# Feed-forward weights turned by DMA transposes instead of TensorE, in a gated cross-attention block

## The chip, the cores and the metric

The kernel runs on one core of a Trainium2 chip. The time is device time in microseconds, as a median over repeated executions of the same program. Engines have short names: PE is TensorE (matmuls), DVE is VectorE, ACT is ScalarE, POOL is GpSimd, and SP is the engine that here only issues DMA transfers. A core also has 16 DMA engines.

## The reference

Sixteen batches of 224 tokens of width 512 attend to 750 context rows of width 384 with 8 heads, and then pass a feed-forward block whose activations and weights are quantised. Both parts are added to the input through a gate.

```python
x = x + tanh(g_xattn) * xattn(layernorm(x), ctx, mask, W_q, W_k, W_v, W_o, b_o)
x = x + tanh(g_ffn) * ffn(layernorm(x), w1, b1, w2, b2)

def weight_quant(w):            # w1 is 2048 x 512, w2 is 512 x 2048
    scale = 1.0 / clip(mean(abs(w)), 1e-5)
    return clip(round(w * scale), -1, 1) / scale

def bitlinear(x, w, b):         # act_quant: rows rounded to 8 bits
    return einsum('bsd,fd->bsf', act_quant(rmsnorm(x)), weight_quant(w)) + b

ffn = lambda x: bitlinear(gelu(bitlinear(x, w1, b1)), w2, b2)
```

The mean of the absolute weights is over the whole matrix, so all of a matrix has to be read before its first element can be rounded. The rounded weights are -1, 0 or 1.

## The kernel before, in words

The work goes batch by batch (the loop over `s` at L1505). For each batch the kept context rows are gathered and turned, keys, values and queries are computed, scores are taken in four units, and each unit passes through a chain of engines: PE computes the scores (L1047), DVE adds the mask and takes the maximum (L1061), ACT takes the exponential and its sum (L1071), DVE inverts the sum (L1080), POOL multiplies (L1081, the product `p`), PE turns the product (L1101 and L1108), and PE weighs the values with it (L1126, L1141). From batch 2 on the output projection (L1189), the first feed-forward matmul (L1259) and the second (L1304) of earlier token tiles are mixed in.

The feed-forward weights are prepared once, beside the first two batches. Each matrix is cut into eight chunks of 128x1024. `load_weights` brings a chunk in as f32 (512 KB; L1349 for w1, L1354 for w2), `sum_weights` adds up its absolute values, on DVE for even chunks and on ACT for odd ones (L1363, L1367), and `scale_weights` makes the scale when all eight are in. `round_weights` then rounds a chunk on DVE in three instructions, L1396 to L1398, the last two of which write a bf16 tile `w16`, taken from three buffers that carry the tag `xq`. `turn_weights` transposes it: eight transposes of 128x128 on PE (L1409 for w1, L1413 for w2) into one accumulator tile `wp`, and one eviction that casts it to fp8 into `w1T` or `w2T`. The accumulator tiles come from `gen`, four buffers that all other matmuls but the scores share.

`evict` (L757) puts each copy out of an accumulator on DVE or ACT, whichever has less planned work at that point; L763 is the copy on DVE, L766 that on ACT. In this program 15 of the 16 casts of turned weights fell to ACT.

`weight_pieces` makes a list of pieces with costs: in step c it rounds chunk c, and turns chunk c - 2. During batch 0 it works on w1, and each round is followed by the load of the same chunk of w2, into the buffer that the rounding has freed, and each turning by the sum over a chunk of w2. During batch 1 it works on w2. `merge` (L1434) mixes three lists, attention, the preparation of the next batch, and this one, so that each advances by the same share of its total cost.

This sets the order in which instructions are emitted. The order on an engine can differ from it, as the trace shows (L1519, emitted for batch 2, runs at 46.93 us, in batch 0): each engine has one queue, and an instruction that waits holds up all that is queued behind it.

The kernel already has transposing transfers on SP's queue: `normalise` turns the quantised activations with one (L1237, bf16, 128x1024, `xqT`), and `gelu` those of the hidden layer (L1288, 128x2048, `hqT`).

Of the kernel before, what the change touches and what calls it, by code (L numbers as in the profile page):

```python
# [9 lines left out]
BF16 = mybir.dt.bfloat16  # L10
# [715 lines left out]
def compact_path(ctx, tc, sh, x, context, out, late_loads):  # L726

    nc = tc.nc
    P = 128
    B, S, D = x.shape  # L730
    _, J, C = context.shape
# [5 lines left out]
    ND = D // P  # L737
# [8 lines left out]
    ident, ident16 = sh.ident, sh.ident16  # L746
    w1T, w2T = sh.w1T, sh.w2T
# [9 lines left out]
    def evict(dst, src, cols):  # L757

        kind = {"saturate": False} if dst.dtype == F8 else {}
        v, s = 80 + 1.2 * cols, 90 + 1.0 * cols  # L760
        if load["v"] + v <= load["s"] + s:
            load["v"] += v
            latest["v"] = nc.vector.tensor_copy(dst, src, **kind).ins  # L763
        else:
            load["s"] += s
            latest["s"] = nc.scalar.copy(dst, src, **kind).ins  # L766

    def gen(shape, dtype, name):
        return ps_gen.tile(shape, dtype, tag="gen", name=name)
# [403 lines left out]
    late = {}  # L1173
# [168 lines left out]
    def load_weights(wi, c):  # L1342

        raws[wi, c] = raw = late["raw"].tile([P, W], F32, tag="raw", name=f"raw_{wi}_{c}", bufs=NPC)
        if wi == 0 and c == 0:

            nc.scalar.copy(raw[0:1, 0:1], live[0]["ctx"][0:1, 0, 0:1])
        if wi == 0:
            return nc.sync.dma_start(  # L1349
                raw.rearrange("p (a d) -> p a d", d=D),  # L1350
                sh.w1_dram[c * 2 * P : (c + 1) * 2 * P, :].rearrange("(a p) d -> p a d", p=P),
            ).ins
        at = c % 2 * W
        return nc.sync.dma_start(raw, sh.w2_dram[c // 2 * P : (c // 2 + 1) * P, at : at + W]).ins  # L1354

    def sum_weights(wi, c):
        if c == 0:
            weight_sums.append(pa.tile([P, NPC], F32, name=f"wsums_{wi}"))
        if c == 1:
            late["junk"] = pa.tile([P, FF], F32, tag="h", name=f"junk_{wi}", bufs=2)  # L1360
        raw = raws[wi, c]
        if c % 2 == 0:
            nc.vector.tensor_reduce(  # L1363
                weight_sums[wi][:, c : c + 1], raw, AX.X, ALU.add, apply_absolute_value=True
            )
        else:
            nc.scalar.activation(late["junk"][:, :W], raw, AF.Abs, accum_out=weight_sums[wi][:, c : c + 1])  # L1367
# [3 lines left out]
    def scale_weights(wi):  # L1371
        tot = small(f"wtot_{wi}")
        nc.vector.tensor_reduce(tot[:, 0:1], weight_sums[wi], AX.X, ALU.add)
        pt = gen([P, 1], F32, f"wtotp_{wi}")
        nc.tensor.matmul(pt, lhsT=sh.ones, rhs=tot[:, 0:1], start=True, stop=True)
        mean = small(f"wmean_{wi}")
        nc.vector.tensor_scalar(mean[:, 0:1], pt, 1.0 / (FF * D), 1e-5, ALU.mult, ALU.max)
        sw = pa.tile([P, 1], F32, name=f"sw_{wi}")
        nc.vector.reciprocal(sw, mean[:, 0:1])
        isw = pa.tile([P, 1], F32, name=f"isw_{wi}")  # L1380
        nc.vector.reciprocal(isw, sw)
        if wi == 0:
            nc.vector.tensor_scalar(isw, isw, 1.0 / 127.0, None, ALU.mult)
        else:

            nc.vector.tensor_scalar(isw, isw, sh.tgates[:, 1:2], 1.0 / 127.0, ALU.mult, ALU.mult)
        weight_scale[wi] = sw
        sh.isw[wi] = isw
# [3 lines left out]
    def round_weights(wi, c):  # L1392

        raw = raws.pop((wi, c))
        quantised[wi, c] = w16 = pa.tile([P, W], BF16, tag="xq", name=f"w16_{wi}_{c}", bufs=3)
        nc.vector.tensor_scalar(raw, raw, weight_scale[wi], 1.0, ALU.mult, ALU.min)  # L1396
        nc.vector.tensor_scalar(w16.bitcast(I16), raw, -1.0, None, ALU.max)
        nc.vector.tensor_copy(w16, w16.bitcast(I16))  # L1398
        load["v"] += 1700

    def turn_weights(wi, c):
        w16 = quantised.pop((wi, c))
        pt = gen([P, 8, P], BF16, f"wp_{wi}_{c}")
        if wi == 0:

            for d in range(ND):
                for a in range(2):
                    at = a * D + d * P
                    nc.tensor.transpose(pt[:, 2 * d + a, :], w16[:, at : at + P], ident16)  # L1409
            evict(w1T[:, :, c * 2 * P : (c + 1) * 2 * P], pt.rearrange("p (d a) f -> p d (a f)", d=ND), 8 * P)  # L1410
        else:
            for f in range(8):
                nc.tensor.transpose(pt[:, f, :], w16[:, f * P : (f + 1) * P], ident16)  # L1413
            f = c % 2 * 8
            evict(w2T[:, f : f + 8, c // 2 * P : (c // 2 + 1) * P], pt, 8 * P)

    def weight_pieces(wi):

        p = []
        if wi == 1:  # L1420
            p += [(0.0, lambda: scale_weights(1))]
        for c in range(NPC + 2):
            if c < NPC:
                p += [(0.2, lambda c=c: round_weights(wi, c))]
                if wi == 0:
                    p += [(0.0, lambda c=c: load_weights(1, c))]
            if c > 1:
                p += [(0.6, lambda c=c: turn_weights(wi, c - 2))]
                if wi == 0:
                    p += [(0.0, lambda c=c: sum_weights(1, c - 2))]  # L1430
        return p
# [73 lines left out]
    for s in range(B):  # L1505
# [8 lines left out]
        if s < 2:  # L1514
            flow = weight_pieces(s)
        else:
            complete = 256 * (projected + 1) <= S * s
            if projected == 0:
                nc.gpsimd.tensor_scalar(sh.bo, sh.bo, sh.tgates[:, 0:1], None, ALU.mult)  # L1519
                nc.gpsimd.tensor_scalar(sh.b2, sh.b2, sh.tgates[:, 1:2], None, ALU.mult)  # L1520
            if complete:
                flow.append((0.0, lambda i=projected: residual(i)))
            if raised < projected:
                flow += up_pieces(raised)
                raised += 1
            if complete:
                flow += project_pieces(projected)
                projected += 1
                if lowered < raised:
                    flow += down_pieces(lowered)  # L1530
                    lowered += 1
# [53 lines left out]
```

## Time and profile before

| what | value |
|---|---|
| median of three runs | 757.25 us (756.26 to 759.62) |
| profiled execution | 755.32 us |
| its span | 753.5 us |
| mean granted PE clock in it | 0.976 |
| casts into w1T on ACT (L766) | 8, from 47.0 to 79.5 us, 1.02 us each |
| casts into w2T | 7 on ACT, 1.02 us each, and 1 on DVE, 1.22 us, from 90.3 to 114.1 us |
| transposes on PE | 64 (L1409) from 46.3 to 78.4 us, 64 (L1413) from 89.2 to 113.7 us, 219 ns each from start to end |

A transpose of 219 ns overlaps the next one, so that eight in a row occupy PE for 0.61 us. In the views of the trace an arrow `out<-in` names the tile written and the tiles read. A wait is named by the waiting instruction and the one that released it. PEld is the load of the stationary operand, which overlaps PE; SPq, POOLq and the like are the queues that issue. The chain is the sequence of work that ended last, followed back from the end of the program.

### The profile page before, as it was taken

The numbers are of one execution on the slowest core, as the hardware profiler recorded it, in microseconds if no ns is written. First come the engines' busy times: TensorE is split into PE (matmuls) and PEld (weight loads), VectorE is DVE, ScalarE is ACT, GpSimd is POOL, SyncE is SP. The second block draws the span as 40 slices with busy tenths as digits, with TensorE's granted clock in tenths as the row PEclk, the third lists the DMA queues.
The fourth block names the chain that finished last, engine by engine and source line by source line (L and its number), as shares of the span: only waits on it lengthen the run. The fifth ranks groups of instructions, "written<-read, shape, count | busy, mean of one in ns | idle before, by whom it ended". The sixth has DMA issues, their size and how long they took to land.

```text
span 753.5 us, 11378 instructions
## 1 busy us (share of the span) xinstructions
PE 680.1 (90%) x3902; PEld 432.9 (57%) x3902; DVE 505.9 (67%) x1300; ACT 407.6 (54%) x960; POOL 397.0 (53%) x543
## 2 busy tenths in 40 slices
PE   4997799999999999997999999999999999988652
PEld 3875587666566566555655575666666666443221
DVE  5598765877484784665768676588594939586860
ACT  1556564384663855736657369266565656460530
POOL 6583567464564644647266564565654453536141
PEclk9998999999999999999999999999999999999887
DMA  6874031132223322222142323123122222213150
GB/s 193 314 267 156 11 90 45 15 73 56 69 47 70 82 56 57 67 57 81 28 99 67 71 67 68 32 77 80 58 57 70 56 70 57 71 28 77 35 113 31
DMA packets 87218, 58.77 MB, mean 78 GB/s; under 512 B 75488, under 2 KB 75632, under 8 KB 87024
## 3 DMA queue, kind: packets, MB, share of 16 engines
q1 hardware_dynamic: 79024, 32.00, 18.8%
q0 software_dynamic: 8128, 25.96, 11.1%
q8 instruction: 33, 0.54, 0.3%
q14 instruction: 33, 0.27, 0.1%
HBM read 32.26 MB, written 7.34 MB: 53 GB/s over the span
## 4 chain that ended last, share of the span: by engine, by line
PE 57%; DVE 12%; issue 10%; POOL 9%; DMA 5%; ACT 2%; POOLq 0%; ACTq 0%; DVEq 0%; SPq 0%
PE qp L1008 9%; PE op L1189 9%; PE fp L1304 8%; PE hp L1259 6%; PE kp L892 5%; PE sim L1047 4%; PE vp L907 4%; PE ptp L1101 3%; PE av L1126 3%; DVE a L1282 2%; POOL p L1081 2%; DVE h L1267 2%; DMA raw<-in_L_ffn_w_dram 2%; DMA hqT<-hq 2%; DVE hq L1285 1%
## 5 line engine op out<-in xcount | busy, mean ns | idle before, releaser
L1081 POOL TENSOR_TENSOR p<-p,rec 112x768 f32<-112x768 f32 (+1 forms) x64 | 84.2, 1318 | 74.8 <-DVE rec L1080 29.6
L1304 PE MATMUL fp<-w2T,hqT 128*128 128x512 fp8e4 x448 | 104.2, 387 | 13.8 <-DMA hqT<-hq 13.7
L1259 PE MATMUL hp<-w1T,xqT 128*128 128x512 fp8e4 x448 | 107.0, 383 | 8.8 <-DVE h L1267 6.2
L1071 ACT ACTIVATE p<-p,nm 112x192 f32<-112x192 f32 (+1 forms) x256 | 106.4, 419 | 11.5 <-DVE nm L1061 11.3
L1008 PE MATMUL qp<-xnT,wq_sb 128*128 128x224 f32 x512 | 104.9, 358 | 0.6 <-ACT xnT L766 0.6
L1189 PE MATMUL op<-wo_sb,xoT 128*128 128x512 f32 x224 | 103.7, 599 | 0.0
L1008 PEld LDWEIGHTS qp<-xnT,wq_sb 128*128 128x128 f32 x512 | 96.8, 193 | 6.4 <-issue 3.3
L1267 DVE SCALAR_TENSOR_TENSOR h<-hp,c,b_bc 128x1024 f32<-128x1024 f32 x56 | 71.6, 1280 | 39.9 <-PE hp L1259 37.4
L1061 DVE CUSTOM_DVE_ANT_0 p<-sim,mask 112x192 f32<-112x192 f32 (+1 forms) x256 | 67.7, 319 | 33.9 <-PE sim L1047 33.4
L1304 PEld LDWEIGHTS <-hqT 128*128 128x128 bf16 x448 | 43.3, 99 | 71.0 <-DMA hqT<-hq 16.9
L1282 DVE TENSOR_REDUCE a<-h 128x1 f32<-128x2048 f32 x28 | 63.9, 2282 | 22.4 <-ACT h L1279 22.3
L1259 PEld LDWEIGHTS <-xqT 128*128 128x128 bf16 x448 | 43.2, 98 | 57.7 <-issue 15.4
L1308 DVE SCALAR_TENSOR_TENSOR y<-fp,c,y 128x512 f32<-128x512 f32 x28 | 20.9, 746 | 76.3 <-PE fp L1304 73.0
L1310 POOL DMA_INDIRECT out_dram<-y,token x28 | 30.9, 1104 | 75.6 <-DVE y L1308 70.6
L1290 ACT ACTIVATE h<-h 128x2048 f32<-128x2048 f32 x28 | 53.4, 1907 | 22.1 <-DVE hq L1285 14.7
L1279 ACT ACTIVATE h<-h 128x2048 f32<-128x2048 f32 x28 | 53.5, 1909 | 19.6 <-DVE k L1200 10.6
L1189 PEld LDWEIGHTS op<-wo_sb,xoT 128*128 128x128 f32 x224 | 40.6, 190 | 38.9 <-issue 36.4
L892 PE MATMUL kp<-ctxT,wk_sb 128*128 128x192 f32 (+1 forms) x384 | 60.9, 306 | 0.0
L892 PEld LDWEIGHTS kp<-ctxT,wk_sb 128*128 128x128 f32 x384 | 55.2, 192 | 6.2 <-issue 4.3
L1247 POOL TENSOR_TENSOR y<-y,b_bc 128x512 f32<-128x512 f32 x28 | 36.6, 1311 | 37.9 <-DVE fx L1228 37.6
L766 ACT COPY pT<-ptp 128x448 f32<-128x448 f32 x63 | 32.7, 536 | 42.6 <-PE ptp L1101 41.3
L1101 PE MATMUL ptp<-ident,p 112*128 112x112 f32 x256 | 36.1, 268 | 17.6 <-POOL p L1081 17.5
(165 smaller groups left out, 1191.4 us busy)
## 6 DMA issues: line engine op xcount, KB each, us to landing
raw<-in_L_ffn_w_dram SPq DMA_DIRECT2D x16, 512.0 KB, 5.6
wq_sb<-in_L_xattn_W_q_dram SPq DMA_DIRECT2D x1, 1024.0 KB, 5.8
b_bc<-in_L_ffn_b_dram SPq DMA_DIRECT2D x1, 1024.0 KB, 7.8
wk_sb<-in_L_xattn_W_k_dram SPq DMA_DIRECT2D x1, 768.0 KB, 7.4
wv_sb<-in_L_xattn_W_v_dram SPq DMA_DIRECT2D x1, 768.0 KB, 8.8
wo_sb<-in_L_xattn_W_o_dram SPq DMA_DIRECT2D x1, 512.0 KB, 3.8
wo_sb<-in_L_xattn_W_o_dram SPq DMA_DIRECT2D x2, 256.0 KB, 5.6
x<-in_x_dram,token POOLq DMA_INDIRECT x28, 3.6
```

The costliest lines, as they stand in the source:

```text
L892: nc.tensor.matmul(pk[:, p - p0, :], lhsT=sh.wk[:, c, p * P : (p + 1) * P], rhs=st["ctxT"][:, c, :cap], start=(c == 0), stop=(c == NC - 1),)
L1008: nc.tensor.matmul(pq[:, i, :], lhsT=sh.wq[:, d, (p + i) * P : (p + i + 1) * P], rhs=st["xnT"][:, d, :], start=(d == 0), stop=(d == ND - 1),)
L1061: nc.vector.tensor_tensor_reduce(out=probs[:, h, :cap], in0=sim[:, j, i, :cap], in1=st["mask"][:, j * begin : j * begin + cap], scale=-(DH ...
L1071: nc.scalar.activation(probs[:, h, :cap], probs[:, h, :cap], AF.Exp, bias=nmax, scale=-1.0, accum_out=total[:TQ, h : h + 1],)
L1081: nc.gpsimd.tensor_tensor(probs[:, :, :cap], probs[:, :, :cap], rec[:TQ].unsqueeze(2).to_broadcast([TQ, 4, cap]), ALU.mult,)
L1101: nc.tensor.transpose(pt[:, h, :], probs[:, h, c : c + P], ident[:TQ, :TQ])
L1189: nc.tensor.matmul(po, lhsT=xoT[:, d, at : at + P], rhs=sh.wo[:, d, :], start=(d == 0), stop=(d == ND - 1))
L1259: nc.tensor.matmul(ph[:, n, :], lhsT=f["xqT"][:, k * ND + d, :], rhs=w1T[:, d, at : at + NB], start=(d == 0), stop=(d == ND - 1),)
L1267: nc.vector.scalar_tensor_tensor(h[:, cols], ph.rearrange("t i n -> t (i n)"), f["c1", k], sh.b1[:, cols], ALU.mult, ALU.add)
L1279: nc.scalar.activation(f["h", k], f["h", k], AF.Gelu)
L1282: nc.vector.tensor_reduce(amax[:, k : k + 1], h, AX.X, ALU.max, apply_absolute_value=True)
L1304: nc.tensor.matmul(po, lhsT=f["hqT", k][:, n, :], rhs=w2T[:, n, :], start=(n == 0), stop=(n == NF - 1))
```

## The change

In `turn_weights` the eight transposes on PE and their accumulator tile go. In their place SP issues one transposing transfer of `w16` into a new bf16 tile `wT` in chip memory, with two buffers in the pool that also holds the raw weights; the cast to fp8 is still placed by `evict` at the same planned cost, and reads `wT`. For w1 the order of the blocks in `wT` differs from that in `wp`, and the view of `w1T` is permuted to match. In `weight_pieces` the cost of turning a chunk goes from 0.6 to 0.2.

```diff
     def turn_weights(wi, c):
         w16 = quantised.pop((wi, c))
-        pt = gen([P, 8, P], BF16, f"wp_{wi}_{c}")
+        wT = late["raw"].tile([P, 8, P], BF16, tag="wT", name=f"wT_{wi}_{c}", bufs=2)
+        nc.sync.dma_start_transpose(out=wT, in_=w16)
         if wi == 0:
 
-            for d in range(ND):
-                for a in range(2):
-                    at = a * D + d * P
-                    nc.tensor.transpose(pt[:, 2 * d + a, :], w16[:, at : at + P], ident16)
-            evict(w1T[:, :, c * 2 * P : (c + 1) * 2 * P], pt.rearrange("p (d a) f -> p d (a f)", d=ND), 8 * P)
+            dst = w1T[:, :, c * 2 * P : (c + 1) * 2 * P].rearrange("p d (a f) -> p a d f", a=2)
+            evict(dst, wT.rearrange("p (a d) f -> p a d f", a=2), 8 * P)
         else:
-            for f in range(8):
-                nc.tensor.transpose(pt[:, f, :], w16[:, f * P : (f + 1) * P], ident16)
             f = c % 2 * 8
-            evict(w2T[:, f : f + 8, c // 2 * P : (c // 2 + 1) * P], pt, 8 * P)
+            evict(w2T[:, f : f + 8, c // 2 * P : (c // 2 + 1) * P], wT, 8 * P)
...
-                p += [(0.6, lambda c=c: turn_weights(wi, c - 2))]
+                p += [(0.2, lambda c=c: turn_weights(wi, c - 2))]
```

## Prediction

> **What bounds the kernel now.** I read the busy lines of the page first, then the 40 slices, then a table of the stretches around the changed code, then the waits of TensorE and the chain. All durations are from the profiled execution.
>
> ```profile
> PE 680.1 (90%) x3902; PEld 432.9 (57%) x3902; DVE 505.9 (67%) x1300; ACT 407.6 (54%) x960; POOL 397.0 (53%) x543
> ...
> PE   4997799999999999997999999999999999988652
> ```
>
> TensorE (PE) is busy 90% of the span, and every slice from the sixth to the thirty-fifth, but one, reads 9. What is late at 117 us is therefore still late at the end, and a microsecond won before 117 us should be carried there. Two neighbouring slices read 7, the fourth and fifth, 57 to 94 us, and this is where the feed-forward weights are prepared. So I cut that time at its events:
>
> ```profile
> 42.00:48.00 6.00, 4.25 (x38) 3.05 (x37) 5.57 (x18) 2.06 (x4) 5.46 (x5) 1.00 1.03 333
> 48.00:57.50 9.50, 9.50 (x74) 8.94 (x73) 9.50 (x28) 8.30 (x26) 9.16 (x6) 1.00 0.59 213
> 57.50:63.00 5.50, 0.42 (x7) 0.25 (x5) 5.50 (x8) 4.51 (x11) 4.71 (x5) 0.89 0.86 254
> 63.00:72.00 9.00, 9.00 (x42) 5.23 (x43) 5.94 (x14) 4.25 (x9) 1.26 (x1) 0.69 0.36 120
> 72.00:80.00 8.00, 8.00 (x78) 6.01 (x76) 4.30 (x12) 6.67 (x15) 1.47 (x1) 1.00 0.15 54
> 80.00:85.00 5.00, 3.88 (x44) 3.01 (x43) 4.04 (x26) 4.05 (x17) 0.90 (x1) 1.00 0.01 2
> 85.00:89.30 4.30, 0.73 (x7) 0.49 (x7) 4.30 (x13) 1.04 (x4) 4.01 (x6) 0.98 0.00 0
> 89.30:98.00 8.70, 8.70 (x58) 7.96 (x59) 8.47 (x20) 5.62 (x14) 7.01 (x6) 0.81 0.32 92
> 98.00:106.00 8.00, 7.84 (x59) 6.54 (x57) 7.78 (x14) 6.12 (x14) 3.29 (x3) 1.00 0.01 4
> 106.00:117.00 11.00, 11.00 (x109) 8.17 (x107) 2.83 (x8) 3.73 (x6) 9.79 (x9) 1.00 0.44 121
> ```
>
> The columns are the stretch, its length, busy time of PE, weight load, VectorE (DVE), ScalarE (ACT) and GpSimd (POOL), the granted clock, the DMA share and GB/s. Batch 0 fills 42 to 85 us, batch 1 fills 85 to 117 us. The reader is to see three things. PE is full in 48 to 57.5, in 63 to 80 and after 106: there a matmul less is time less. PE is nearly empty in 57.5 to 63 and in 85 to 89.3. And DVE is full from 42 to 63 and from 85 to 106: there DVE may be the bound and PE's idle time only its shadow. TensorE's waits in that time:
>
> ```profile
> PE ptp L1101 <- POOL p L1081: 5.1, 1, 5.1
> PE wp L1413 <- DVE w L1398: 3.6, 1, 3.6
> PE wp L1409 <- DVE w L1398: 1.7, 1, 1.7
> ```
>
> Two of the three are the transposes that the change removes: they stand at the head of PE's queue and wait for the first rounded chunk, 3.6 us for w2 and 1.7 us for w1.
>
> **What the Trainium skill says.** "VectorE: DVE Perf Modes", section "The three transpose paths", puts a 128x128 bf16 transpose at 390 ns on TensorE and 1309 ns in the DMA crossbar. The trace agrees in direction only: eight pipelined TensorE transposes occupy PE for 0.61 us together, and the crossbar transfer of a whole 128x1024 chunk lands 3.1 us after issue. "DMA: Bandwidth & Descriptors", section "Queues, rings and completion order", says that each engine takes descriptors in ring order, so a transpose issued behind a 512 KB load on SP's queue waits for it; no row of the kernel before has the two together. "TensorE: Matmul & The Clock Gate", section "Why this matters for your kernels", advises no PE gap over about 3 us, or the clock falls; the trace agrees, with 0.69 granted after the 5.5 us gap.
>
> **Removed: 128 transposes on PE.** They are 16 groups of eight. On the chain of the program a group costs 0.45 us at full clock and up to 1.03 us at a low one. In batch 0 the chain holds 0.62, 0.45, 0.45, 0.85, 0.45 and 1.00 us (the last is two groups), together 3.8 us; in batch 1 it holds 1.03, 0.45, 0.45, 0.45 and 1.00 us, together 3.4 us. The whole is 7.2 us at most. The two waits add up to 5.2 us, and one cast of w2T (L766) is on the chain with 0.94 us, because the attention's transposes wait for its PSUM buffer. The ceiling of the change is 7.2 + 5.2 + 0.9 = 13.3 us.
>
> **How much of it is free, batch 0.** Up to the end of the query matmuls at 57.4 us PE loses one wait and three groups: 1.7 + 0.62 + 0.45 + 0.45 = 3.2 us. What is late next is POOL: its fetch of x at 57.66 us waits for that query matmul, three further DMA issues follow, and only then the product p (L1081) at 61.36 us, for which PE stands still. The sums that p needs were ready at 55.25 us and 59.09 us. With the fetch 3.2 us earlier the first p starts near 58.2 us, and PE restarts near 59.7 us: the gain passes through. From 63 to 80 us PE is full and loses 0.85 + 0.45 + 1.00 = 2.3 us. Batch 0 gives 5.5 us if the added waits cost nothing.
>
> **Batch 1.** Without the wait PE has the transposes of the context and the keys to do at 85.7 us. But p of the third and fourth score units comes from DVE, ACT and POOL: the reduction L1061 runs at 94.9 us, its sums end at 99.9 us, the product ends after 101.7 us and PE turns it at 103.3 us. L1061 there waited 0.2 us only, so DVE, full of rounding, sets it. If the order of PE's queue stays, the 3.6 us and the 1.9 us of groups ahead of it are hidden by DVE and only the groups after 103.9 us count: 0.45 + 1.00 = 1.45 us. If values and queries (2.7 + 3.1 us, at 104 to 110 us) are put ahead of the late p, up to 5.5 us more are won. The order isn't that of the code: L1519, emitted for batch 2, runs at 46.93 us. I take 3.0 us of the 1.45 to 7.9 us.
>
> **Added: 16 transposing transfers on SP.** The row to price them is the same shape:
>
> ```profile
> L1237 SPq DMA_TRANSPOSE xqT<-xq x15: 1190/1238/2390, 144.6 to 700.2; - x15
> ...
> DMA to landing us min/median/max: 2.4/3.1/4.6
> ```
>
> Issue takes 1.24 us of SP, 16 x 1.24 = 20 us in 70 us, where SP does nothing else but eight loads of w2 (0.33 us each), so SP has room. The loads of w2 stand in the same queue in batch 0; they land in 3.8 to 7.1 us (median 5.2), and DMA is full from 42 to 48 us (1.03). A transpose right behind one lands between 3.1 us and 7.1 + 3.1 = 10.2 us after it is ready; my estimate is 6 us. In batch 1 no load is left and I take 3.1 us. Three waits are new. The cast on ACT waits for the landing, and behind it in ACT are exponentials and evictions, for which PE and POOL wait. Rounding on DVE (L1397) reuses one of three bf16 buffers, which is now free only when the transfer of three chunks ago has landed; chunks 0 to 3 were rounded at 44.6, 46.2, 47.8 and 49.4 us, so with 6 us from 46.3 us the fourth stands until about 52.3 us, 2.9 us, with the L1061 of units 2 and 3 behind it. And SP's next load waits behind a transpose; its sums are read two chunks later, so this cover is wide (one wait of 0.6 us in the kernel before). Lower bound of all three: nothing, where other ready work is put ahead; upper bound: the third rival below. I charge 2.0 us, since p has 6.1 and 2.3 us between its sums and its start.
>
> **Edits with one answer.** The casts stay on ACT (15 x 1.02 us; one on DVE, 1.22 us). From chip memory ACT took 1.06 us for 128x1024 f32 (L1367), so 15 x 0.04 = 0.6 us more at most, beside PE. DVE lies between 0.41 us (L1398) and 1.22 us; I keep 1.22. The accumulator buffers come free earlier, which is the 0.9 us above. The weight 0.2 for 0.6 moves the first turning from 9% to 19% of the batch and the last from 91% to 94%: nothing, with the reordering in the range.
>
> **Sum.** 5.5 + 3.0 - 2.0 = 6.5 us. Against the profiled execution of 755.3 us (span 753.5 and 1.8 around it) this is 748.8 us; the median of the runs is 757.25 us, 1.9 us above, so the forecast is 750.7 us, with 747 to 753.4 as this case's own range.
>
> **Rivals.** *All of it is won*: PE's queue is refilled in batch 1 and the waits are covered: 13.3 us, 744.0 us. For it: PE has ready work in both gaps. Against: DVE is full there. *Hidden*: DVE and the p chain set both batches, and only the groups in 63 to 80 and after 106 us count, less the 2.0 us: 2.3 + 1.45 - 2.0 = 1.8 us, 755.5 us. For it: DVE at 5.50 of 5.50 and 4.30 of 4.30 us. *Slower: the three bf16 buffers.* Each of the rounds 3 to 7 in batch 0 waits on DVE for a landing behind a load. At 10.2 us, less two rounds of 1.6 us, the first stands 7.0 us, and the four after it I put at 2.5 us each, together 17 us, of which DVE, being full until 63 us but not after it (5.94 of 9.00 us), absorbs the last two: 12 us on the path, against 6.5 + 2.0 = 8.5 us won, with another 2 us for ACT's casts: 5.5 us slower, 762.8 us. It decides once the landings cost more than 8.5 us on the path, about 2 us for each of batch 0's first four waits. Against it: the rounds are spread over the batch and can be put behind other DVE work.
>
> **Numbers.** Chances: the forecast 0.44, all won 0.16, hidden 0.20, slower 0.20. About 0.5%, 3.8 us, is what can be told from no change, so faster 0.60, within 0.20, slower 0.20. The range 743 to 759.5 us leaves out most of the slower case and part of the largest gain.
>
> **What would show it.** Right: PE about 10 us less busy, no wait of PE on L1398, the gap at 57 us closed by some 3 us, PE filled at 85 us, and after 120 us the same picture some 6 us earlier. Right on the waits: ACT's casts waiting on DMA wT for 0 to 3 us, landings near 6 us in batch 0. Wrong: L1397 waiting on wT's transfer for more than 3 us at a time, a PE gap above 5.5 us, or later stages reordered so that the shift at 117 us isn't the shift at the end.

## The result and the profile after

| | before | after |
|---|---|---|
| median of five runs on the same chip | 757.25 us | 768.36 us |
| ratio of after to before | | 1.0156, 95% interval 1.0133 to 1.0179 |
| profiled execution, and its span | 755.32 us, 753.5 us | 769.74 us, 767.8 us |
| mean granted PE clock | 0.976 | 0.956 |

The change makes the kernel 11 us slower. The forecast was 750.7 us, faster, and the range ended at 759.5 us. These are the lines of the page after that answer to those shown of before, with the row of the granted clock:

```profile
PE 684.9 (89%) x3774; PEld 435.8 (57%) x3774; DVE 501.1 (65%) x1298; ACT 408.5 (53%) x962; POOL 397.8 (52%) x543
...
PE   4998687999989999997999999999999999988642
...
PEclk9978898999999999999899999999999999999877
```

The 128 matmuls are gone (3774 instead of 3902), but PE is busy 4.8 us longer, at a lower mean clock (0.956 for 0.976). The fourth to seventh slices now read 8, 6, 8 and 7 where they read 7, 7, 9 and 9: the hole has moved to the right. The same stretches as in the prediction, of the kernel after, with the same columns:

```profile
42.00:48.00 6.00, 6.00 (x35) 4.16 (x32) 4.43 (x14) 1.31 (x3) 5.36 (x7) 0.50 1.04 310
48.00:57.50 9.50, 9.36 (x48) 9.04 (x47) 8.34 (x26) 6.11 (x19) 8.43 (x7) 0.78 1.02 265
57.50:63.00 5.50, 2.87 (x21) 1.88 (x19) 5.50 (x7) 5.33 (x15) 4.63 (x3) 0.95 0.53 167
63.00:72.00 9.00, 8.99 (x26) 5.63 (x27) 9.00 (x20) 3.84 (x7) 0.00 (x0) 0.65 0.84 209
72.00:80.00 8.00, 7.68 (x76) 5.18 (x76) 4.08 (x16) 4.82 (x8) 0.00 (x0) 1.00 0.85 153
80.00:85.00 5.00, 1.40 (x16) 0.79 (x12) 3.40 (x23) 5.00 (x16) 1.47 (x1) 1.00 0.98 166
85.00:89.30 4.30, 1.65 (x7) 1.36 (x7) 1.31 (x8) 4.03 (x16) 1.62 (x2) 0.65 0.00 0
89.30:98.00 8.70, 7.48 (x39) 6.88 (x39) 8.70 (x25) 5.35 (x14) 8.03 (x7) 0.78 0.43 81
98.00:106.00 8.00, 4.79 (x29) 4.23 (x28) 5.03 (x11) 4.76 (x12) 7.10 (x5) 1.00 0.76 167
106.00:117.00 11.00, 11.00 (x80) 7.36 (x78) 3.75 (x7) 5.53 (x8) 0.00 (x0) 1.00 0.43 82
```

PE is busier in 57.5 to 63 (2.87 us of work for 0.42). But 80 to 85 is now nearly empty (1.40 for 3.88), and so is part of 98 to 106 (4.79 for 7.84). In the last row POOL does nothing at all for 11 us (0.00 for 9.79), while PE is full. That idle POOL is one of the two things that the next views follow.

To see where the time goes I compare one marker, the start of the matmul L1141 of each batch, in both traces. After stands to before by -2.7 us in batch 0, +1.9 in batch 1, +8.5 in batch 2, +8.5, +8.7 and +8.6 in batches 3 to 5, +10.3 in batch 6, +13.3 in batch 7, and +14.3 us at the end of the span. The marker of batch 0 is indeed early. Two places lose it: one just after the batch 0 marker, and one between those of batches 1 and 2. A third loss, 4.7 us after batch 5, is taken up under "Left open" below.

**First loss, 80 to 88 us.** TensorE's waits of the kernel after, from 42 to 135 us:

```profile
PE ptp L1101 <- POOL p L1081: 11.1, 5, 5.2
PE wtotp L1375 <- DVE wtot L1373: 6.0, 1, 6.0
PE kp L892 <- ACT pT L766: 1.2, 1, 1.2
```

Both waits for a rounded chunk (L1398) are gone, as forecast. In their place PE waits 6.0 us for the sum of w2 (1.1 us before), from which the scale of w2 is made. The marker L1375 is 2.8 us late, so that 5.6 us are lost here after the batch 0 marker. PE arrives 2.1 us earlier than before (it stops at 81.6 us, 83.7 before), and the sum comes 3.0 us later (87.47 us, 84.51 before): the longer wait is in part PE's own lead, given up.

One thing that is later is the loads. SP's queue of the kernel after (start, duration of the group, queue):

```profile
46.96 4.70 SPq L1354 DMA_DIRECT2D raw<-in_L_ffn_w_dram  x3
51.77 3.88 SPq L1404 DMA_TRANSPOSE wT<-w  x2
60.99 0.99 SPq L1354 DMA_DIRECT2D raw<-in_L_ffn_w_dram  x2
...
77.79 0.33 SPq L1354 DMA_DIRECT2D raw<-in_L_ffn_w_dram  x1
```

Loads and transposes alternate in one queue. The last load of w2 is issued at 77.79 us, where the kernel before issued it at 70.40 us. A load needs the raw buffer that a rounding frees, a rounding needs one of the three bf16 buffers, and a bf16 buffer is free when its transfer has landed. These are roundings and the total on DVE of the kernel after:

```profile
59.42 1.54 DVE L1397 TENSOR_SCALAR w<-raw 128x1024 int16<-128x1024 f32 x1
...
77.08 0.68 DVE L1397 TENSOR_SCALAR w<-raw 128x1024 int16<-128x1024 f32 x1
87.24 0.18 DVE L1080 RECIPROCAL rec<-sum 112x4 f32<-112x4 f32 x1 [2.30 <-ACT p L1071]
87.47 0.13 DVE L1373 TENSOR_REDUCE wtot<-wsums 128x1 f32<-128x8 f32 x1
```

The fourth rounding starts at 59.42 us (49.41 before) and the eighth at 77.08 (69.69). Each load is issued within 0.1 us of the end of the rounding that frees its buffer, so DVE dates the loads, not the transfers ahead of them in SP's queue. Only 0.2 us of DVE's idle time is put down to a transfer of wT: DVE doesn't stand still for it, the rounding merely comes later in its order, and the load behind it too.

The late load alone doesn't make PE wait. Two of the experiments below have no transfer in batch 0 and issue the last load just as late (78.23 us in e4, 77.65 us in e2). Their totals come even later, at 89.72 and 89.13 us, and PE waits only 1.1 us there. What ends last in the change is ACT:

```profile
82.86 1.04 ACT L1367 ACTIVATE junk<-raw 128x1024 f32<-128x1024 f32 x1
83.90 1.98 ACT L766 CAST w1T<-wT 128x1024 fp8e4<-128x1024 bf16 x2
85.78 0.46 ACT L1071 ACTIVATE p<-p,nm 112x192 f32<-112x192 f32 x1
```

The last sum over w2 (L1367) is done at 84.0 us. The total still stands 3.5 us in DVE's queue: ahead of it is the reciprocal L1080, which waits for exponentials on ACT, and these stand behind the last two casts of w1. The casts could hardly run earlier, since the last two transfers of w1 landed near 83.8 and 84.7 us; in the kernel before the same two casts ran at 78.57 us. This chain is read from the trace. No run moved these casts. The transfers themselves are as cheap as estimated:

```profile
L1404 SPq DMA_TRANSPOSE wT<-w x16: 1232/1237/3408, 51.8 to 112.4; - x16
...
DMA to landing us min/median/max: 3.0/4.3/6.1
```

**Second loss, 105 to 130 us.** POOL of the kernel before (start, duration, instruction, idle time before it and its releaser):

```profile
105.45 1.29 POOL L793 DMA_INDIRECT y<-in_x_dram,token  x1 [2.82 <-DVE w L1397]
...
120.59 1.26 POOL L1182 TENSOR_TENSOR y<-y,bo_bc 128x512 f32<-128x512 f32 x1 [1.20 <-DMA y<-in_x_dram,token]
121.81 2.89 POOL L1081 TENSOR_TENSOR p<-p,rec 112x768 f32<-112x768 f32 x2
```

POOL of the kernel after:

```profile
117.02 1.04 POOL L793 DMA_INDIRECT y<-in_x_dram,token  x1 [11.29 <-DVE xoT L763]
...
126.21 2.48 POOL L1182 TENSOR_TENSOR y<-y,bo_bc 128x512 f32<-128x512 f32 x2
128.65 1.46 POOL L1081 TENSOR_TENSOR p<-p,rec 112x768 f32<-112x768 f32 x1
```

`residual` (L1178 to L1182) fetches the tiles `y` for the output projection and adds a bias to them: six fetches and six additions, 16 us of POOL from first to last in the kernel before, where all of them stand ahead of the first products `p` of batch 2. After, five fetches and four additions do. The tiles `y` live in the pool `rows`, which takes the memory of the pool `raw` when that is closed (L1535, L1536). So the first fetch waits for the last reader of `raw`. Before, that is the last rounding of w2 (`DVE w L1397`). After, `wT` lives in `raw` too, and the last reader is a cast of w2T out of `wT`:

```profile
115.56 0.69 DVE L763 CAST w2T<-wT 128x1024 fp8e4<-128x1024 bf16 x1 [2.70 <-DMA wT<-w]
```

It ends on DVE at 116.25 us; DVE's queue had stood 2.7 us for its transfer. (The view names the next copy on DVE, of `xoT`, as the releaser. In e6 below, where this cast falls to ACT, it names the cast itself.) The fetch starts 11.6 us later than before, and p of batch 2 6.8 us later. PE, which never waited there before, now stands 5.2 us for p, and the marker falls back by another 6.6 us.

### The profile page after: what moved, and what is told of

The parts are those of the page before. It is cut to its first block, busy times and chain, and to the rows that moved or that the text cites. A ratio compares the mean times of both kernels' runs of the same rounds, so it can differ in the third digit from the quotient of the medians.

```text
span 767.8 us, 11154 instructions
## 1 busy us (share of the span) xinstructions
PE 684.9 (89%) x3774; PEld 435.8 (57%) x3774; DVE 501.1 (65%) x1298; ACT 408.5 (53%) x962; POOL 397.8 (52%) x543
## 4 chain that ended last, share of the span: by engine, by line
PE 53%; DVE 11%; POOL 11%; issue 10%; DMA 7%; ACT 4%; POOLq 0%; ACTq 0%; DVEq 0%; SPq 0%
PE qp L1008 8%; PE op L1189 8%; PE fp L1304 8%; PE hp L1259 6%; PE kp L892 5%; PE vp L907 4%; PE sim L1047 4%; POOL p L1081 3%; PE ptp L1101 3%; DVE a L1282 2%; DMA raw<-in_L_ffn_w_dram 2%; PE av L1126 2%; DVE h L1267 2%; DMA hqT<-hq 2%; DMA wT<-w 2%
## 5 line engine op out<-in xcount | busy, mean ns | idle before, releaser
L1008 PE MATMUL qp<-xnT,wq_sb 128*128 128x224 f32 x512 | 109.4, 369 | 0.6 <-ACT xnT L766 0.6
L1008 PEld LDWEIGHTS qp<-xnT,wq_sb 128*128 128x128 f32 x512 | 100.8, 200 | 8.6 <-issue 4.4
L892 PE MATMUL kp<-ctxT,wk_sb 128*128 128x192 f32 (+1 forms) x384 | 64.9, 319 | 1.4 <-ACT pT L766 1.2
L892 PEld LDWEIGHTS kp<-ctxT,wk_sb 128*128 128x128 f32 x384 | 59.1, 202 | 7.8 <-issue 4.3
```

The costliest lines, as they stand in the source:

```text
L892: nc.tensor.matmul(pk[:, p - p0, :], lhsT=sh.wk[:, c, p * P : (p + 1) * P], rhs=st["ctxT"][:, c, :cap], start=(c == 0), stop=(c == NC - 1),)
L1008: nc.tensor.matmul(pq[:, i, :], lhsT=sh.wq[:, d, (p + i) * P : (p + i + 1) * P], rhs=st["xnT"][:, d, :], start=(d == 0), stop=(d == ND - 1),)
```

## The experiments

My theory after this reading: (a) the shared memory delays POOL's fetch of y, (b) the late sums of w2 cost some 5 us, (c) what the removed transposes win is lost again at POOL. Rivals: the emission order that follows from the cost 0.2, the transfers of w1 alone, and the transfers of w2 alone. Every ratio is to the kernel before on the same chip, with its 95% interval. The time given is the median of all executions, and the ratio leaves some of them out, so the two don't always divide exactly. "Marker" is L1141 against the kernel before, in the profiled execution.

**e1: wT in memory of its own.**

```diff
-        wT = late["raw"].tile([P, 8, P], BF16, tag="wT", ...)
+        wT = pa.tile([P, 8, P], BF16, tag="wT", ...)
```

> The changed kernel with the two wT buffers in the persistent pool instead of the pool whose memory the token tiles y take over after batch 1. Theory A (the fetch of y on POOL waits for the last cast from wT, and the product p of batch 2 stands behind it): the first fetch of y moves from 117.0 to about 108 us, TensorE's wait of 5.2 us at 125 us goes, and the time falls by 6 to 7 us to about 762 us. Rival B (the loss is made in batch 0, by the three bf16 buffers and the loads behind transposes on SP): the time stays within 2 us of 768 us.

Measured: 765.91 us, 1.0096 (1.0060 to 1.0132). Against the change's 1.0156, sharing the memory costs about 0.6%, and the rest of the loss stays. The fetch of y starts at 111.55 us. The profiled execution was one of the two longest of fourteen (span 769.6 us), so I use the ratio and not its markers.

**e2: only w2 by transfer, w1 on PE** (cost 0.2, `wT` in `raw`).

```diff
     def turn_weights(wi, c):
+        if wi == 1:
+            return turn_by_dma(wi, c)
```

> w1 is turned on TensorE as before, w2 by transposing transfers into wT in the shared pool as in the change. Theory A: batch 0 is as before, but y still waits for the last wT, so about 6 us above the kernel before, 763 us. Rival B: with nothing added to batch 0 the loss is gone, 757 us or less.

Measured: 765.67 us, 1.0075 (1.0025 to 1.0125). PE's wait for the sum is back at 1.1 us. POOL's y waits 14.3 us, for the last cast on DVE as in the change, and PE waits 14.8 us in all for p from 42 to 135 us. Much of that comes with the cost 0.2: e4, which has no transfers, has 11.1 us of it.

**e3: only w1 by transfer, w2 on PE** (cost 0.2).

```diff
     def turn_weights(wi, c):
+        if wi == 0:
+            return turn_by_dma(wi, c)
```

> w1 is turned by transposing transfers, w2 on TensorE as before. Theory A: the last cast from wT is done by 90 us, y does not wait for it, and only what batch 0 loses is left, 757 to 760 us. Rival B: batch 0 carries the loss, 764 us or more, and TensorE waits about 6 us for the total of w2's sums at 82 us.

Measured: 766.34 us, 1.0129 (1.0062 to 1.0196). Here the wait for the sum is 6.0 us and y is released by the rounding (`DVE w L1397`), at 110.06 us. So (b) belongs to the transfers of w1, and (a) to those of w2. Each half alone is slower than the kernel before. Both halves have the cost 0.2 in them, though, which alone loses 0.4% (e4): beyond that, e2's 0.75% isn't clear of the intervals.

**e4: only the cost, 0.2 for 0.6, in the kernel before.**

```diff
-                p += [(0.6, lambda c=c: turn_weights(wi, c - 2))]
+                p += [(0.2, lambda c=c: turn_weights(wi, c - 2))]
```

> The kernel before with only the planned cost of turning a chunk changed from 0.6 to 0.2. Theories A and B: no loss from the order, within 2 us of 757 us. Rival C (the order of emission alone makes the loss, by where rounds stand against score units on VectorE): 763 us or more.

Measured: 762.50 us, 1.0041 (1.0011 to 1.0072). The order by itself, with the transposes on PE, loses 0.4%. TensorE's waits of this kernel from 42 to 135 us:

```profile
PE ptp L1101 <- POOL p L1081: 11.1, 3, 8.0
PE wtotp L1375 <- DVE wtot L1373: 1.1, 1, 1.1
```

The 3.6 us wait for a rounded chunk of w2 has gone down to 0.7 us, and PE waits 8.0 us for one p, that of batch 0 (5.1 before). The last rounding of w1 runs at 77.51 us instead of 69.69 us, and with it the last load of w2. The marker is +4.8 us in batch 0 and +5.1 in batch 2.

**e5: the kernel before, with its hand-over of memory delayed.** A tile of 4 bytes per partition in `raw`, which ACT writes after the last cast into w2T, lets y wait as in the change; nothing else differs.

```diff
+            if c == NPC - 1:
+                hold = late["raw"].tile([P, 1], F32, tag="hold", name="hold", bufs=1)
+                nc.scalar.copy(hold[0:1], w2T[0:1, f, c // 2 * P : c // 2 * P + 1])
```

> The kernel before (transposes on TensorE, cost 0.6) with one more tile of 4 bytes a partition in the pool of the raw weights, written by ACT with one element after the last cast of w2, so that the memory of that pool comes free at the last cast and not at the last rounding. Theory A: the first fetch of y on POOL moves from 105.5 to about 115 us, the product p of batch 2 and TensorE behind it move with it, 5 to 7 us slower than the kernel before (ratio 1.007 to 1.009). Rival B (the shared memory matters only by chance of the order in the changed kernel): within 2 us of the kernel before.

Measured: 765.66 us, 1.0159 (1.0115 to 1.0203), as slow as the change itself. Its POOL:

```profile
115.05 1.05 POOL L793 DMA_INDIRECT y<-in_x_dram,token  x1 [12.48 <-ACT hold L1418]
```

The markers are -0.7 and -0.5 us in batches 0 and 1, then +5.8 in batch 2 and +6.6 in batch 7, and the span is 759.9 us. This is the second loss alone, shown without the change. Its size is less sure: the ratio is larger than this one trace gives (6.4 of 753.5 us, 0.8%).

**e6: the change with the cost left at 0.6.** The diff is that of the change without its last two lines.

> The changed kernel with the planned cost of turning back at 0.6. If the order of emission gives the 0.4% that the cost alone gave with TensorE's transposes, the changed kernel falls by about 3 us to ratio 1.011 or 1.012. If the order matters only for transposes that stand in TensorE's queue, it stays at 1.015.

Measured: 766.41 us, 1.0152 (1.0106 to 1.0198). The old cost doesn't help here: 5.4 us at the sum, and y waits 10.6 us for the last cast, which is now on ACT. The 0.4% of e4 doesn't show in the change.

**e7: both, memory of its own and the cost 0.6.**

> The changed kernel with wT in memory of its own and the cost at 0.6: both suspected losses undone. Theory A with the order: 1.009 less 0.004, 1.003 to 1.006. If the transposing transfers cost by themselves (late landings ahead of evictions, the sums of w2 late), it stays at 1.008 or more.

Measured: 762.05 us, 1.0121 (1.0060 to 1.0181). The trace shows (a) gone, y at 108.20 us, and (b) left with 4.8 us at the sum; the marker is 0.0, +3.7 and +2.9 us in batches 0 to 2 and +3.6 in batch 7. The times are slower than I expected of that, and against e6 memory of its own brings only 0.3%, within the intervals.

**e8: no turning at all.** The kernel before, cast straight from the bf16 tile; the stored weights are then not transposed.

```diff
-        pt = gen([P, 8, P], BF16, f"wp_{wi}_{c}")
...
-            for f in range(8):
-                nc.tensor.transpose(pt[:, f, :], w16[:, f * P : (f + 1) * P], ident16)
-            evict(w2T[:, f : f + 8, c // 2 * P : (c // 2 + 1) * P], pt, 8 * P)
+            evict(w2T[:, f : f + 8, c // 2 * P : (c // 2 + 1) * P], w16.rearrange("p (a f) -> p a f", a=8), 8 * P)
```

> The kernel before with the turning left out altogether: the rounded chunk is cast as it lies, so the stored weights are not transposed and the output is another one. It prices what can be won at all by taking the 128 transposes off TensorE with nothing in their place. My prediction's working says 6.5 us plus the 2.0 us of waits that it charged, 8.5 us, and 13.3 us at most: ratio 0.982 to 0.989. The rival, that VectorE and the chain of p set batches 0 and 1: 2 to 4 us, ratio 0.995 to 0.998.

Measured: 758.09 us, 1.0038 (1.0015 to 1.0061). This is the run that decides most. All 128 transposes are gone and no transfer stands in their place, and the kernel isn't faster. (One thing beside it differs: a bf16 tile is now freed by its cast, not by the transposes.) POOL of this kernel, and its two longest waits of TensorE up to 135 us:

```profile
105.77 1.59 POOL L793 DMA_INDIRECT y<-in_x_dram,token  x1 [5.87 <-DVE w L1397]
...
121.21 1.26 POOL L1182 TENSOR_TENSOR y<-y,bo_bc 128x512 f32<-128x512 f32 x1 [1.18 <-DVE y L1192]
122.43 2.89 POOL L1081 TENSOR_TENSOR p<-p,rec 112x768 f32<-112x768 f32 x2
```

```profile
63.89 1.01 PE L1101 MATMUL ptp<-ident,p 112*128 112x112 f32 x4 [7.49 <-POOL p L1081]
...
123.95 0.45 PE L1101 MATMUL ptp<-ident,p 112*128 112x112 f32 x1 [4.73 <-POOL p L1081]
```

At the marker of batch 1 PE is 3.3 us ahead (108.63 for 111.89 us). The fetch of y can't follow: it starts at 105.77 us (105.45 before), when the last rounding of w2 on DVE releases the memory, and DVE rounds no earlier than before. Sixteen microseconds of y later, p starts at 122.43 us (121.81 before). PE arrives early and waits 4.7 us, where it didn't wait before. (The 7.5 us are in batch 0.) So the lead is gone, and the marker of batch 2 is 2.6 us late; PE's work and the clock in 117 to 160 us go from the first of these lines (the kernel before) to the second (e8):

```profile
117.00:160.00 43.00, 42.90 (x270) 30.13 (x268) 29.32 (x99) 21.92 (x70) 26.53 (x30) 1.00 0.18 36
```

```profile
117.00:160.00 43.00, 38.27 (x239) 28.72 (x238) 28.24 (x83) 15.77 (x50) 24.73 (x28) 0.92 0.17 32
```

**e9 to e12: each y behind the last p emitted.** Four kernels, in which the fetch and the addition of the first three y are bound behind the last product that was emitted before them.

```diff
+        with ExitStack() as behind:
+            if i < 3:
+                behind.enter_context(tc.issue_after(last_p[0]))
             for k in range(2):
                 fetch_x(y[:, k, :], 2 * i + k)
```

e9 is e8 (again with the turning left out) with this edit, e10 the kernel before, e11 the kernel e7, and e12 the kernel e7 with w1 turned on PE.

> As the kernel without any turning (stored weights are not transposed, another output), and the first three fetches of y on POOL are put behind the product p of the batch in which they are emitted. Theory A (what removing the transposes wins is lost again because POOL fetches y, from the last rounding at 105 us, for 16 us ahead of the first p of batch 2): TensorE's wait of 7.5 us for p goes, the lead of 3 to 4 us at 112 us is kept or grows, and the time falls by 6 to 9 us against the kernel without turning, to ratio 0.992 to 0.996. Rival (VectorE and the clock set these batches whatever POOL does): stays at 1.002 or more.

> The kernel before with the same order of y on POOL. Theory A: there p of batch 2 came just as TensorE was free (no wait at 123 us), so within 0.3% of the kernel before, or up to 0.4% faster from p of units 2 and 3.

> The changed kernel with wT in memory of its own, cost 0.6 and y behind p. Theory A with the loss in batch 0 left (TensorE waits 4.8 us at 83 us for w2's sums, which the transposing transfers and the three bf16 buffers make late): up to 3 us better than without y behind p, ratio 0.999 to 1.004. If the late landings of wT ahead of evictions are the loss: stays at 1.006 or more.

> As the last one, but w1 is turned on TensorE as before and only w2 by transposing transfers. With batch 0 as in the kernel before, the wait for w2's sums is back to 1.1 us: ratio 0.992 to 0.998, the fastest of those that compute the reference. Rival (transposing transfers cost in batch 1 as well): 1.000 or more.

Measured: e9 763.23 us, 1.0075 (1.0050 to 1.0100); e10 767.69 us, 1.0158 (1.0099 to 1.0218); e11 774.64 us, 1.0201 (1.0146 to 1.0256); e12 767.65 us, 1.0116 (1.0068 to 1.0164). None is faster than the kernel before; my expectations of a gain in e9 and e12, and of no change in e10, were wrong. In batch 2 e9 did as expected: p runs at 112.80 us, and the marker is 4.3 us ahead of the kernel before. But later y now run in batches 3 and 4 (from 153 and 203 us), and the lead is gone by batch 4 (+1.2 us). There PE waits 2.5 us for DVE near 164 us and 3.5 us for p near 226 us. The base e10 has nearly the same waits (2.5 and 3.3 us), so this is the price of the binding and not a loss of the lead: e9 stays ahead of e10 by 4.5 us at the marker of batch 1 and by 5.1 to 5.4 us at those of batches 2 to 7, though by only 1.8 us at the end of the span. In the ratios e9 is 0.8% faster than e10. This is weak, because e10's executions run from 762.7 to 775.6 us; without its two longest the means are 765.6 us for e10 and 763.6 us for e9, 0.3% apart.

**e13 to e15: all three y behind the last p of batch 1**, so that they stay in batch 2. e13 is e8 with this edit, e14 the kernel before, e15 the kernel e7.

```diff
+        if i == 0:
+            late["p"] = last_p[0]
...
+                behind.enter_context(tc.issue_after(late["p"]))
```

> The kernel before with the turning left out as before (the stored weights are not transposed), and the first three fetches and additions of y bound to come behind the last product p of batch 1, so that they no longer stand ahead of batch 2's first products as in the run with the turning alone left out (1.0038), but can still run inside batch 2. Theory (the lead won in the preparation is lost at POOL, where y and p share one queue, wherever y is put): POOL's 16 us of y still lie ahead of some p of batch 2 or 3, a wait of TensorE for p of 4 to 7 us stays, and the end is not ahead of the kernel before by over 2 us: ratio 0.998 to 1.006. Rival (only the place of y_0 ahead of batch 2's first p loses it): TensorE stays 3 to 5 us ahead to the end, ratio 0.993 to 0.996.

> The kernel before with that same binding of y alone, as the base of the run without the turning. Theory: it moves POOL's work and wins nothing: 1.000 to 1.008. Rival: 0.995 to 0.999. The difference between the run without the turning and this one is what 128 transposes are worth when y is out of the way of batch 2's first products: theory up to 2 us, rival 4 to 6 us.

> The change with memory of its own for wT, the cost kept at 0.6, and that same binding of y. Theory: as the same without the binding (1.012), 1.008 to 1.016, since the wait of about 5 us for the sums of w2 and the waits on DVE's last casts are not touched by it. Rival (y is all that is lost): 0.996 to 1.002.

Measured: e13 763.01 us, 1.0102 (1.0050 to 1.0154); e14 771.27 us, 1.0199 (1.0148 to 1.0249); e15 773.79 us, 1.0249 (1.0182 to 1.0315). As the theory had it, POOL's y is in the way of some p here too. POOL of e13, in which p of the third unit of batch 2 comes after the last four additions:

```profile
114.09 1.47 POOL L1082 TENSOR_TENSOR p<-p,rec 112x768 f32<-112x768 f32 x1 [14.80 <-DVE rec L1081]
...
133.64 4.91 POOL L1188 TENSOR_TENSOR y<-y,bo_bc 128x512 f32<-128x512 f32 x4
138.51 2.88 POOL L1082 TENSOR_TENSOR p<-p,rec 112x768 f32<-112x768 f32 x2
```

The wait of PE for this p is 7.4 us in e13 and in e14 alike. Both theories missed the size: all three are slower than either allowed, and between e13 and e14 lie 8.3 us (1.0%), more than the 2 us of the theory or the 4 to 6 us of the rival. The lead of e13 over e14 is 4.2 us at the marker of batch 1, 5.5 at that of batch 2, 5.4 at that of batch 4, and 8.4 at that of batch 7: here it is carried. (From 5.4 to 8.4 it grows where e14 loses time of its own, see "Left open".) So the theory must be put more narrowly. The y work is in the way wherever it is put, but a lead is lost to it only where its start is fixed by something that did not get earlier, as in e8 by DVE's last rounding. Where y is bound to p, which moves along with PE, the lead passes, though in kernels that are themselves 1.6 to 2.0% slower than the kernel before.

## Why the prediction was wrong

**The step that failed** is the one that multiplies everything else: "What is late at 117 us is therefore still late at the end, and a microsecond won before 117 us should be carried there." It holds for what is late (e5 is 5.8 us late at the marker of batch 2 and 6.4 us at the end), and not for what is early. The busy share of PE after 117 us (42.90 of 43.00 us) told that PE had no slack, and I took that as proof that nothing else had a date of its own. In the kernel before, p of batch 2 starts at 121.81 us on a POOL that is full from 105 us on, with a fetch that waits for DVE's rounding. PE comes just when p is ready. e8 shows it without any transfer: 3.3 us ahead in batch 1, 2.6 us behind in batch 2. With y out of the way (e9) PE is still 4.3 us ahead in batch 2. I did not ask what dates POOL's fetch of y at 105 us, though the last row of my own table gave POOL 9.79 of 11.00 us.

**Batch 0 failed in the same way: of its 5.5 us, leaving out the transposes gives nothing.** The prediction read POOL's fetch of x at 57.66 us as waiting for the query matmul, and let PE's gain pass through it: "With the fetch 3.2 us earlier the first p starts near 58.2 us". In e8, without the groups and the wait, PE comes to this p at 56.4 us (57.8 before) and stands 7.5 us (5.1 before). Its POOL:

```profile
58.28 1.00 POOL L793 DMA_INDIRECT x<-in_x_dram,token  x1 [0.30 <-issue]
...
62.36 2.89 POOL L1081 TENSOR_TENSOR p<-p,rec 112x768 f32<-112x768 f32 x2
```

POOL's own queue, full from 43 us on, dates this fetch. The 0.31 us for which it stood in the kernel before is no longer than the 0.30 us with which the fetch after it follows as "issue". The first p starts at 62.36 us in e8, 61.64 us in e9 and 61.50 us in e13, against 61.36 us before, and the markers of batch 0 are +1.5, -0.4 and +0.9 us. The change's own -2.7 us, and its smaller gap at 57 us, have another origin, so that the right sign here is luck. Its first p starts 2.4 us earlier, at 58.92 us, on a POOL whose multiplication of `bo_bc` (L1519, L1515 after) took 1.69 us where it took 4.52 us in the kernel before and in e8. Why it was shorter isn't known.

**Batch 1 was sized about right.** Its 3.0 us stand beside 3.7 us in e8 (from +0.45 at L1375 to -3.3 us at the marker) and 0.9 us in the change itself (from +2.8 to +1.9). (The upper end of the range there, 7.9 us, is 1.45 + 5.5 and the 0.94 us of the cast, which isn't said.) So at the end of batch 1 the lead was 3.3 us in e8, 5.2 in e9 and 3.9 in e13, where the prediction without the added waits has 8.5 us. The ceiling of 13.3 us was never reached; the largest gain that any pair showed is 8.3 us.

**Another step that failed isn't in the sum:** where `wT` lives. It makes y wait for the last cast, and e5 shows this alone as 1.6% in the times and 5.8 us at the marker. Giving `wT` memory of its own brings back less, 0.6% in e1 and 0.3% in e7, so the cause is shown and its size is not settled.

**The charge of 2.0 us for added waits was too small, and the place was wrong.** I looked for DVE's roundings to stand and held SP's loads to be covered ("its sums are read two chunks later, so this cover is wide"). DVE stood 0.2 us for a bf16 buffer, and the late loads alone did no harm (e2, e4). PE's wait for the total of w2 grew from 1.1 to 6.0 us, so that 4.9 us are lost in batch 0 alone, part of it PE's lead and part of it casts on ACT with exponentials behind them, a wait that the prediction named and gave no size of its own. With memory of its own, cost 0.6 and the same placing of y, the kernel with the transfers is slower than the one with no turning at all by 1.5% (e15 to e13) and 1.3% (e11 to e9), some 10 us, and in both pairs no execution of the one reaches the other. Against transposes on PE the transfers are 0.5% slower (e15 to e14) or 0.4% (e11 to e10), and intervals near 0.5% each don't settle that.

**"PE about 10 us less busy" was wrong**, since the same matmuls take longer at a lower clock. The clock was 0.80 in 42 to 85 us (0.92 before). Part of this is no effect of the change: in e5, which differs from the kernel before only after batch 1, the clock was 0.50 in 42 to 48 us as well, as in the change.

**The cost 0.2, put at "nothing"**, is 0.4% by itself (e4), where it moves the last rounding of w1 by 7.8 us, and nothing that can be told in the change (1.0156 with it, 1.0152 without).

**The small terms held.** Issue took 1.24 us as taken. Landing had a median of 5.4 us in batch 0 and 3.1 us in batch 1, where I took 6 us and 3.1 us. The order in which descriptors are taken, which the prediction cited, doesn't by itself say that a transfer lands after the load ahead of it; here it did: the last load of w2 landed at 81.9 us, and the transfer issued behind it at 83.8 us. An ACT cast from chip memory took 1.045 us for 1.06. The one DVE cast took 0.69 us, where I kept 1.22. The low price that the Trainium skill ("VectorE: DVE Perf Modes", "The three transpose paths") gives TensorE's transposes, 390 ns against 1309 ns in the DMA crossbar, points the right way here: eight took 0.61 us on PE, a transfer of the same chunk 4.3 us to land.

**The rivals.** The slower one had the right side and the wrong mechanism: it let DVE stand for the three bf16 buffers, 7.0 us the first time, where DVE stood 0.2 us in all and the roundings came later in its order, as that rival's own "against it" allowed. "Hidden" named DVE and the p chain as what sets both batches, and e8 is nearest to it, though even slower (1.0038, where without the charge of 2.0 us it has 3.75 us of gain, 0.995). What hides the gain is POOL: its own queue ahead of the first p of batch 0, and y ahead of p in batch 2, neither of which it named. Two of the prediction's own signs of being wrong came true: a PE gap above 5.5 us, and a shift at 117 us that isn't the shift at the end.

**Left open.** After batch 5 the change loses another 4.7 us up to the marker of batch 7. The waits there are for p, 1.7 and 4.9 us in sum (1.6 and 3.7 before), and the clock falls with them: it was 0.50 in 315.0 to 318.4 and in 366.2 to 373.0 us, where the kernel before has one such stretch, 351.9 to 355.3 us (0.51). e14 has no transfers, and it loses the same 4.7 us there, with the same two stretches (0.51 and 0.50). So this loss doesn't need the transfers; why it comes in some kernels isn't known. No version that was tried beats the kernel before. A larger set of bf16 buffers, another queue for the transfers and another place for the casts on ACT weren't tried.

## What to carry to other kernels

A lead is worth something only if each thing that a later stage waits for gets earlier too: follow every queue beyond the edited stage to the first instruction whose start is fixed by another engine, and ask when that comes. A new tile in a pool that is closed and handed on moves the date at which the next pool's first tiles may be written, so name the last reader of the pool before and after. When the trace names a releaser, look at the length of the wait: one that is no longer than the gap with which the instructions of that engine follow each other anyway doesn't tell what sets its time. And when a transfer replaces matmuls, ask which engine reads what it brings, and what stands behind that reader in its queue.

## What was not expected of the hardware

- A wait can cost more than its length: with the 6.0 us wait that ended at 87.65 us the granted clock went to 0.50 in 86.3 to 93.1 us, and with the 4.7 us wait of e8 that ended at 123.95 us it was 0.50 in 121.8 to 128.6 us, so that 117 to 160 us had 0.92 where it was 1.00. This agrees with the Trainium skill ("TensorE: Matmul & The Clock Gate", "Why this matters for your kernels"), which advises against PE gaps of over about 3 us.
- A cast of 128x1024 bf16 to fp8 out of chip memory took 0.69 us on DVE and 1.045 us on ACT; out of an accumulator it had been 1.22 us on DVE and 1.02 us on ACT.
- Eight transposing transfers, 0.26 MB each, raised the mean busy share of the DMA engines in 42 to 85 us from 0.49 to 0.89.
